# Two edits at the end of a two-layer block: the last chunk of the experts turned on TensorE, and token arrays stored in DRAM as they lie in SBUF

## The chip, the cores and the metric

The kernel runs on one core of one Trainium2 chip. A core has five engines, each with its own queue of instructions, worked through in order: TensorE (PE in the profile; PEld is its weight load), VectorE (DVE), ScalarE (ACT), GpSimd (POOL) and SyncE (SP), which here mostly issues DMAs. The on-chip memories are SBUF (128 partitions) and PSUM, where TensorE writes its results. DRAM is reached by DMA only, over 16 DMA engines that all queues share. The metric is the device time in microseconds of one execution.

## The reference, cut to what matters

The input `x` has 8 sequences of 512 tokens of 256 features. The block has two layers, each adding to `x` the sum of an attention and a second part, both fed from the normalised `xn`.

```python
xn = _layernorm(x, axis=-1)
x = x + _L0_attn_ref(xn, ...) + _L0_ffn_ref(xn, ...)     # causal attention; gated feed-forward, 1024 wide
xn = _layernorm(x, axis=-1)
x = x + _L1_attn_ref(xn, ...) + _L1_ffn_ref(xn, ...)     # attention with position bias; experts
```

The experts of layer 1, where the larger edit lies:

```python
grouped = x.reshape(x.shape[:-2] + (-1, ne, d))              # groups of 16 tokens
logits = jnp.einsum('...btd,des->...btes', grouped, controller)
perm = (logits + tie == max over the 16 tokens of the group) # one token per group, expert and slot
sel = jnp.einsum('...btd,...btes->...besd', grouped, perm)   # the token picked: 64 (expert, slot) pairs
inner = jax.nn.relu(jnp.einsum('...besd,desf->...besf', sel, f1) + bias)   # 256 -> 64
inter = jnp.einsum('...besf,esfd->...besd', inner, f2)                     # 64 -> 256
out = jnp.einsum('...besd,...btes->...btd', inter, perm)     # back to the token's place
```

All 64 pairs of expert and slot have weights of their own, so `inner` and `inter` are computed pair by pair over many groups, while `sel` and `out` go group by group over all pairs.

## The kernel before, in words

**Stages.** Layer 0's attention comes first, then the feed-forward of layer 0 (which also prepares the first sequence of layer 1), layer 1's attention, and the experts. Between the stages, and where SBUF is short, arrays lie in DRAM: `x1d` (x after layer 0's attention), `x2d` (after its feed-forward), `x3d` (after layer 1's attention), `xn1d` (layer 1's `xn`), and `xnd` and `xt1d` (`xn` of the two layers, transposed).

**Token arrays.** A sequence in SBUF is a tile of 128 partitions by 4 by 256: token `t * 128 + p` lies on partition `p`, at place `t`. `x1d`, `x2d`, `x3d` and `xn1d` are 4096 rows of 256 floats, token by token, so the 4 KB of a partition go to or come from four places of 1 KB each. `xnd` and `xt1d` are kept partition by partition, 4 KB in one piece. `fetch_x` (L82), `leave_x` (L86), the store of `xn1d` in `prep1` (L536), `fetch_xn` (L940) and the load of `x` in `combine` (L1118, two of the four places, 256 KB) move the token arrays. In one execution either arm of the feed-forward runs, and there are 8 stores of each array, 8 loads of `x1d`, 16 of `x2d`, 8 of `xn1d` and 16 half loads of `x3d`.

**The experts** go in four chunks of two sequences, 64 groups each (`NG`); the 64 pairs are 32 pairs of pairs (`NP`), two of 64 hidden features together filling 128 rows.

- `route(b)`: logits by TensorE, the maximum by VectorE, `perm` and its transpose `permT`.
- `gather(b)`: `sel`, features on partitions, by products with a block-diagonal `perm`.
- `up(ch)` (L1050): `inner` = relu of 64-wide products, 128 of them, over `sel`; the result is laid block-diagonally, so that one product holds two pairs.
- `go_down(ch)` (L1082): 32 products `d_ps` (L1092), 128 rows of (pair, group) by 256 features, evicted to `down`. Now rows stand by pair and group, and `combine` needs, for each group, all pairs on the partitions. The turn is made through DRAM: 8 stores `inter<-down` (L1102) and 8 loads `back<-inter` (L1108), each 512 KB.
- `combine(ch)` (L1110): for two token tiles at a time, loads `x` from `x3d`, 8 products `y_ps` (L1122) of `permT` with `back`, an addition (L1130), and the store to `out` (L1131).

**Buffers.** The pool `big` has one buffer for each tag: `sel` (read by `up`) and `back` (read by `combine`), 32 KB for each partition both. So `back` of a chunk is written only when the `combine` of the chunk ahead has read its own. In PSUM `ps_a` has 3 buffers, `ps_b` 3 and `ps_c` 2 (for `y_ps`); `x` in `combine` has 3 in SBUF. `evacuate` (L71) takes VectorE and ScalarE in turn.

**Order.** The attention stages are written in an order of their own, kept as written. In the experts, functions are generators interleaved by `by_turns`; a scheduler then sets the order of the instructions on each engine. Of `up(3)` with `combine(2)`, and then `go_down(3)`, it makes on TensorE: `up(3)`, 18 products of `go_down(3)`, `combine(2)`, 14 products, `combine(3)`.

Of the kernel before, what the change touches and what calls it, by code (L numbers as in the profile page):

```python
# [2 lines left out]

# [1 line left out]

# [6 lines left out]
F32 = mybir.dt.float32  # L12
# [9 lines left out]
P = 128  # L22
B, S, D = 8, 512, 256
NT = B * S // P
TPB = S // P
# [37 lines left out]
def block_kernel(ctx: ExitStack, tc: tile.TileContext, a: dict, out: bass.AP):  # L63
# [7 lines left out]
    def evacuate(dst, src):  # L71

        turn[0] ^= 1
        if turn[0]:
            nc.vector.tensor_copy(dst, src)
        else:
            nc.scalar.copy(dst, src)
# [3 lines left out]

    def fetch_x(pool, b, src, tag="x", to=x):  # L82
        to[b] = pool.tile([P, TPB, D], F32, tag=tag, name="x")
        nc.sync.dma_start(to[b], src[b * S : (b + 1) * S, :].rearrange("(t p) d -> p t d", p=P))

    def leave_x(b, dst):  # L86
        nc.sync.dma_start(dst[b * S : (b + 1) * S, :].rearrange("(t p) d -> p t d", p=P), x[b])

    x1d = dram.tile([B * S, D], F32, name="x1d")
    x2d = dram.tile([B * S, D], F32, name="x2d")  # L90
    x3d = dram.tile([B * S, D], F32, name="x3d")
    xnd = dram.tile([B * P, 2 * S], F32, name="xnd")
    xn1d = dram.tile([B * S, D], F32, name="xn1d")
    xt1d = dram.tile([B * P, 2 * S], F32, name="xt1d")

    cst = cpool.tile([P, C_CAUSAL], F32, name="cst")
# [432 lines left out]
    def prep1(b, xn, pools, psum, tag, wqkv, bufs, evacuate):  # L529


        for t in range(TPB):
            normalise(1, b, t, xn[:, t, :], xn)
            if t % 2:
                yield
        nc.sync.dma_start(xn1d[b * S : (b + 1) * S, :].rearrange("(t p) d -> p t d", p=P), xn)  # L536
        yield
        yield from pause()
        xt = pools[0].tile([P, 2, S], F32, tag="xT", name="xT")
        for i in range(0, TPB, 2):  # L540
            yield from transpose_steps(
                [xn[:, i + j, :] for j in range(2)], xt[:, :, i * P : (i + 2) * P], psum, tag, evacuate
            )
        yield xt
        yield from pause()
        for m in range(2):
            for kind, dst, scale in ((0, qd1, -(HD**-0.5)), (1, kd1, 1.0)):
                cols = slice(kind * D + m * P, kind * D + (m + 1) * P)
                yield from project(
                    pools[1],  # L550
                    psum,
                    tag,
                    [(wqkv[:, k, cols], xt[:, k, :]) for k in range(2)],
                    scale,
                    dst[b, m],
                    (lambda: ready1.add((b, m))) if kind else None,
                    not kind,
                    bufs,
                )
# [371 lines left out]
    with ExitStack() as st:  # L931
# [7 lines left out]

        def fetch_xn(b):  # L940
            t = work.tile([P, TPB, D], F32, tag="xn", name="xn1")
            nc.sync.dma_start(t, xn1d[b * S : (b + 1) * S, :].rearrange("(t p) d -> p t d", p=P))
            return t

        def fetch_xt(b):
# [27 lines left out]
        inner = big.tile([P, NP, 2, NG], F32, name="inner")  # L973
        nc.gpsimd.memset(inner[:ES, :, 1, :], 0.0)
        nc.gpsimd.memset(inner[ES:, :, 0, :], 0.0)
        perms, permT, sel, back = {}, {}, {}, {}

        def route(b):

# [73 lines left out]
        def up(ch):  # L1053

            s = sel.pop(ch)
            for q in range(4):
                u_ps = ps_b.tile([P, NP // 4, NG], F32, tag="b", name="u_ps")
                for r in range(NP // 4):
                    for k in range(2):
                        for e in range(2):  # L1060
                            nc.tensor.matmul(
                                u_ps[e * ESZ : (e + 1) * ESZ, r, :],
                                lhsT=f1[q][:, k, (2 * r + e) * ESZ : (2 * r + e + 1) * ESZ],
                                rhs=s[:, k, q * NP // 2 + 2 * r + e, :],
                                start=(k == 0),
                                stop=(k == 1),
                            )
                    if r % 2:
                        yield
                at = slice(q * NP // 4, (q + 1) * NP // 4)  # L1070
                raw = work.tile([P, NP // 4, NG], F32, tag="raw", name="raw")
                nc.vector.tensor_tensor(raw, u_ps, fbias[:, at].unsqueeze(2).to_broadcast([P, NP // 4, NG]), ALU.add)
                yield
                for e in range(2):
                    half = slice(e * ES, (e + 1) * ES)
                    nc.scalar.activation(inner[half, at, e, :], raw[half], AF.Relu)
                yield
# [3 lines left out]
        def go_down(ch):  # L1081

            back[ch] = big.tile([P, NG // 2, D], F32, tag="back", name="back")
            for r0 in range(0, NP, NR):
                if r0 % NH == 0:
                    half = dram.tile([P, NH, D], F32, name=f"inter{ch}_{r0}")
                down = work.tile([P, NR, D], F32, tag="down", name="down", bufs=3)
                for r1 in range(0, NR, 2):
                    d_ps = ps_b.tile([P, 2, D], F32, tag="b", name="d_ps")
                    for i in range(2):  # L1090
                        r = r0 + r1 + i
                        nc.tensor.matmul(  # L1092
                            d_ps[:, i, :],
                            lhsT=inner[:, r].rearrange("p e g -> p (e g)"),
                            rhs=f2[r // (NP // 4)][:, r % (NP // 4), :],
                            start=True,
                            stop=True,
                        )
                    yield
                    evacuate(down[:, r1 : r1 + 2, :], d_ps)  # L1100
                    yield
                nc.sync.dma_start(half[:, r0 % NH : r0 % NH + NR, :], down)  # L1102
                if (r0 + NR) % NH == 0:
                    by_group = half.rearrange("(e g h) r d -> h e r g d", e=2, h=2)
                    for h in range(2):
                        for e in range(2):
                            at = h * ES + 2 * (r0 + NR - NH) + e
                            nc.sync.dma_start(back[ch][at : at + 2 * NH - 1 : 2], by_group[h, e])  # L1108

        def combine(ch):  # L1110

            rows, pt = back.pop(ch), permT.pop(ch)
            for i in range(2):
                b = 2 * ch + i
                for t in range(0, TPB, 2):
                    at = slice(b * S + t * P, b * S + (t + 2) * P)
                    xr = work.tile([P, 2, D], F32, tag="x", name="x", bufs=3)
                    nc.sync.dma_start(xr, x3d[at, :].rearrange("(t p) d -> p t d", p=P))  # L1118
                    y_ps = ps_c.tile([P, 2, D], F32, tag="y", name="y_ps")
                    for j in range(2):  # L1120
                        for q in range(4):
                            nc.tensor.matmul(  # L1122
                                y_ps[32 * q : 32 * q + 32, j, :],
                                lhsT=pt[:, i, (t + j) * P + 32 * q : (t + j) * P + 32 * q + 32],
                                rhs=rows[:, (i * TPB + t + j) * 4 + q, :],
                                start=True,
                                stop=True,
                            )
                        yield
                    nc.vector.tensor_add(xr, xr, y_ps)  # L1130
                    nc.sync.dma_start(out[at, :].rearrange("(t p) d -> p t d", p=P), xr)  # L1131
                    yield

        def by_turns(*works):
            works = deque(w for w in works if w is not None)
            while works:
                w = works.popleft()
                try:
                    next(w)
                    works.append(w)  # L1140
                except StopIteration:
                    pass

        def chain(*works):
            for w in works:
                yield from w
# [3 lines left out]
        by_turns(chain(gather(0), gather(1)))  # L1150
        for ch in range(chunks):
            more = ch + 1 < chunks
            by_turns(
                up(ch),
                chain(
                    *([route(2 * ch + 2), route(2 * ch + 3)] if more else []),
                    *([combine(ch - 1)] if ch else []),
                ),
            )
            by_turns(go_down(ch), chain(gather(2 * ch + 2), gather(2 * ch + 3)) if more else None)  # L1160
        by_turns(combine(chunks - 1))


# [51 lines left out]
```

## Time and profile before

The program was timed three times: 2200.61, 2200.88 and 2191.32 us, median 2200.61.

| | |
|---|---|
| time of the profiled execution | 2195.91 us |
| its span in the profile | 2194.2 us |
| instructions | 29805 |
| TensorE busy | 1930.5 us, 88% of the span |
| VectorE, ScalarE, GpSimd busy | 1337.9, 938.8, 610.1 us |
| DMA packets, bytes | 151905, 254.40 MB |
| the experts' stage | about 1940 to 2194 us |
| `up(3)` ends on TensorE | 2124.0 us |

All times in the profile count from the span's start. An engine that is busy most of the span isn't the bound in every stage; the chain of waits, followed back from the last instruction, shows which work or transfer each stretch waited for. The page's rows of tenths give the busy share of each of 40 slices of 55 us. The granted clock is that of TensorE as a share of full speed. Products of f32 appear as two records each in the trace, transposes as one.

### The profile page before, as it was taken

What the parts mean: (1) busy time and instruction counts of PE and PEld (TensorE: products, weight loads), DVE (VectorE), ACT (ScalarE), POOL (GpSimd) and SP (SyncE); (2) the same over time, 40 slices, a digit from 0 to 9 for tenths busy, and PEclk for the clock granted to TensorE, in tenths of its full rate; (3) what the DMA queues carried; (4) which work ended last, traced back from release to release, by engine and by line L of the source; (5) the groups of instructions that cost most, each with busy time, mean ns of one, the idle gap of its engine ahead of it and who ended that gap; (6) DMA issues with size and microseconds to landing.
All of it is one profiled execution on the core that took longest, in us unless ns stands there. A gap on an engine that the chain in (4) does not pass through costs nothing.

```text
span 2194.2 us, 29805 instructions
## 1 busy us (share of the span) xinstructions
PE 1930.5 (88%) x10182; PEld 1259.3 (57%) x10182; DVE 1337.9 (61%) x3621; ACT 938.8 (43%) x1570; POOL 610.1 (28%) x552
## 2 busy tenths in 40 slices
PE   3689999999799999999999779999999999968863
PEld 1345555555488888888888544544544444436652
DVE  3667776677345535535535367888878878735431
ACT  0244444445322212212222137777777778834320
POOL 4211111112100000000000256656656657732200
PEclk8799999999899999999999879999999999989986
DMA  5647767674430000000001384554553554167697
GB/s 126 177 121 175 185 164 195 174 173 109 181 127 30 20 10 29 20 1 20 20 1 49 90 238 98 117 124 91 116 127 89 114 121 77 47 235 204 192 254 204
DMA packets 151905, 254.40 MB, mean 116 GB/s; under 512 B 14382, under 2 KB 84911, under 8 KB 151395
## 3 DMA queue, kind: packets, MB, share of 16 engines
q1 hardware_dynamic: 146418, 245.56, 43.2%
q10 hardware_dynamic: 4864, 6.24, 0.9%
q8 instruction: 82, 1.34, 0.3%
q0 software_dynamic: 464, 0.63, 0.1%
q14 instruction: 77, 0.62, 0.1%
HBM read 171.58 MB, written 91.29 MB: 120 GB/s over the span
## 4 chain that ended last, share of the span: by engine, by line
PE 62%; DMA 12%; DVE 10%; ACT 4%; issue 4%; POOL 1%; SPq 1%; ACTq 1%; POOLq 0%; DVEq 0%
PE hid_ps L780 21%; PE t_ps L338 7%; PE ctx_ps L385 7%; PE s_ps L287 6%; PE proj_ps L522 3%; DMA qs<-rows 3%; DVE junk L299 3%; DMA ks<-kd 3%; PE val L780 3%; PE gate L780 3%; PE ffo L780 2%; PE o_ps L443 2%; DMA back<-inter 1%; DMA inter<-down 1%; PE d_ps L1092 1%
## 5 line engine op out<-in xcount | busy, mean ns | idle before, releaser
L287 PE MATMUL s_ps<-ks,qs 96*128 96x512 f32 (+2 forms) x1024 | 471.0, 468 | 81.6 <-DMA ks<-kd 40.4
L351 POOL TENSOR_TENSOR pt<-pt,bias 128x512 f32<-128x512 f32 x320 | 408.8, 1288 | 242.5 <-ACT pt L350 233.5
L338 PE MATMUL t_ps<-qs,ks 128*128 128x512 f32 (+2 forms) x1024 | 394.8, 391 | 38.1 <-DMA qs<-rows 15.1
L299 DVE CUSTOM_DVE_ANT_0 junk<-s_ps,bias 128x512 f32<-128x512 f32 x512 | 338.0, 686 | 120.3 <-PE s_ps L287 107.2
L287 PEld LDWEIGHTS s_ps<-ks,qs 96*128 96x128 f32 x1024 | 201.9, 198 | 265.6 <-DVE least L299 110.7
L299 DVE CUSTOM_DVE_ANT_0 junk<-s_ps,mask 128x384 f32<-128x384 f32 (+3 forms) x512 | 233.1, 486 | 142.0 <-PE s_ps L287 140.8
L338 PEld LDWEIGHTS t_ps<-qs,ks 128*128 128x128 f32 x1024 | 197.9, 195 | 149.1 <-ACT pt L350 43.2
L376 ACT ACTIVATE pt<-pt 128x1024 f32<-128x1024 f32 x256 | 273.7, 1069 | 3.2 <-POOL pt L351 3.1
L770 DVE CAST h<-hf 128x512 fp32r<-128x512 f32 x192 | 81.2, 426 | 303.2 <-ACT hf L819 302.2
L385 PE MATMUL ctx_ps<-pt,vst 128*32 128x512 f32 (+3 forms) x2048 | 262.5, 533 | 3.7 <-ACT pt L376 2.5
L819 ACT ACTIVATE hf<-hid_ps,sh 128x512 f32<-128x512 f32 x128 | 88.1, 688 | 380.5 <-PE hid_ps L780 374.6
L350 ACT COPY pt<-t_ps 128x512 f32<-128x512 f32 x320 | 184.3, 585 | 151.8 <-PE t_ps L338 150.3
L780 PE MATMUL hid_ps<-h,h1T_m 128*128 128x512 f32 x1024 | 237.4, 391 | 0.0
L780 PE MATMUL hid_ps<-h,h2T_m 128*128 128x512 f32 x1024 | 236.9, 392 | 0.0
L780 PEld LDWEIGHTS hid_ps<-h,h2T_m 128*128 128x128 f32 x1024 | 192.2, 188 | 42.6 <-issue 2.9
L780 PEld LDWEIGHTS hid_ps<-h,h1T_m 128*128 128x128 f32 x1024 | 191.2, 188 | 43.8 <-DVE h L771 2.5
L128 POOL TENSOR_TENSOR r<-ve,power 128x4 f32<-128x4 f32 x16 | 16.2, 1012 | 706.9 <-DVE ve L125 602.9
L363 POOL TENSOR_SCALAR_AFFINE_SELECT pt<-pt 128x512 f32<-128x512 f32 x128 | 81.7, 639 | 404.6 <-ACT pt L353 229.6
L353 ACT ACTIVATE pt<-t_ps 128x512 f32<-128x512 f32 (+1 forms) x256 | 130.3, 546 | 99.9 <-PE t_ps L338 95.0
L348 DVE TENSOR_TENSOR pt<-t_ps,bias 128x512 f32<-128x512 f32 x192 | 131.6, 685 | 15.4 <-PE t_ps L338 14.0
L771 DVE TENSOR_TENSOR h<-hf,h 128x512 fp32r<-128x512 f32 x192 | 132.0, 690 | 5.6
L355 ACT ACTIVATE pt<-t_ps 128x256 f32<-128x256 f32 (+1 forms) x128 | 61.9, 491 | 148.3 <-PE t_ps L338 117.1
(137 smaller groups left out, 2265.2 us busy)
## 6 DMA issues: line engine op xcount, KB each, us to landing
qs<-qd SPq DMA_DIRECT2D x128, 256.0 KB
ks<-kd SPq DMA_DIRECT2D x64, 256.0 KB
ks<-kd SPq DMA_DIRECT2D x128, 128.0 KB
inter<-down SPq DMA_DIRECT2D x32, 512.0 KB
back<-inter SPq DMA_DIRECT2D x32, 512.0 KB
qd<-hi SPq DMA_DIRECT2D x32, 256.0 KB
qd<-lo SPq DMA_DIRECT2D x32, 256.0 KB
kd<-hi SPq DMA_DIRECT2D x32, 256.0 KB
```

Source lines behind the costliest of these rows:

```text
L287: nc.tensor.matmul(ps[:, :n], lhsT=job["qs"][:ROW_M, r, c * P : (c + 1) * P], rhs=job["ks"][:ROW_M, r, :n], start=True, stop=True,)
L299: nc.vector.tensor_tensor_reduce(junk[:, :width], ps[:, :width], add, 1.0, 3e38, ALU.add, ALU.min, job["least"][:, c, r : r + 1])
L338: nc.tensor.matmul(ps[:, base - at : S - at], lhsT=job["ks"][:, r, j * P : (j + 1) * P], rhs=job["qs"][:, r, base:], start=True, stop=True,)
L348: nc.vector.tensor_tensor(pt[:, r, :], ps, bias, ALU.add)
L350: nc.scalar.copy(pt[:, r, :], ps)
L351: nc.gpsimd.tensor_tensor(pt[:, r, :], pt[:, r, :], bias, ALU.add)
L353: nc.scalar.activation(pt[:, r, lo:], ps[:, lo:], AF.Exp, scale=-1.0)
L376: nc.scalar.activation(pt, pt, AF.Exp, scale=-1.0)
L385: nc.tensor.matmul(job["ctx"][32 * r : 32 * r + 32, lo:], lhsT=job["v"][:, j, r, :], rhs=job["p"][j][:, r, lo:], start=(j == 0), stop=(j = ...
L771: nc.vector.tensor_tensor(t[1][:, k, :], value, t[0][:, k, :].bitcast(F32), ALU.subtract)
L780: nc.tensor.matmul(ps, lhsT=l, rhs=r, start=(i == 0), stop=(i == len(pairs) - 1))
L819: nc.scalar.activation(hf, ps, AF.Gelu, scale=scales[sc][:, o : o + 1])
```

## The change

**The last chunk** (`ch` = 3) no longer goes through DRAM. `go_down_here` computes the products the other way round: weights `f2` stationary, `inner` moving (128 columns: two pairs of 64 groups), two halves of 128 features, so 64 products of 128 columns in place of 32 of 256. The result has features on partitions; its evictions write it to `dn` with the pairs innermost, in the buffer of `sel`, which `up(3)` has read by then. `turn_here` transposes 128 by 128 blocks of `dn` on TensorE (64 transposes, 16 groups of four in a PSUM buffer of `ps_a`), which gives rows by (group of two, pair) with features along, and evicts them to `back`. `combine` draws these steps as it goes, 12 before its first tile and 8 before the others. `combine(2)` is now chained behind `go_down_here(3)` in place of beside `up(3)`. The other chunks are as before.

**The layouts.** `x1d`, `x2d`, `x3d` and `xn1d` become 1024 rows (sequence, partition) of 1024 floats, as the tiles lie in SBUF; `tokens` picks the view by the array's width, so the input `x` and the output keep theirs.

```diff
     def fetch_x(pool, b, src, tag="x", to=x):
         to[b] = pool.tile([P, TPB, D], F32, tag=tag, name="x")
-        nc.sync.dma_start(to[b], src[b * S : (b + 1) * S, :].rearrange("(t p) d -> p t d", p=P))
+        nc.sync.dma_start(to[b], tokens(src, b))
...
+    def tokens(src, b):
+
+        if src.shape[1] == D:
+            return src[b * S : (b + 1) * S, :].rearrange("(t p) d -> p t d", p=P)
+        return src[b * P : (b + 1) * P, :].rearrange("p (t d) -> p t d", d=D)
+
+    x1d = dram.tile([B * P, TPB * D], F32, name="x1d")
+    x2d = dram.tile([B * P, TPB * D], F32, name="x2d")
+    x3d = dram.tile([B * P, TPB * D], F32, name="x3d")
...
+    xn1d = dram.tile([B * P, TPB * D], F32, name="xn1d")
...
+        def go_down_here(ch):
+
+            dn = turned[ch] = big.tile([P, 2, NG, ES], F32, tag="sel", name="dn")
+            for r0 in range(0, NP, 4):
+                for d in range(2):
+                    d_ps = ps_b.tile([P, 8, NG], F32, tag="b", name="d_ps")
+                    for r in range(r0, r0 + 4):
+                        nc.tensor.matmul(
+                            d_ps[:, 2 * (r - r0) : 2 * (r - r0) + 2, :],
+                            lhsT=f2[r // (NP // 4)][:, r % (NP // 4), d * P : (d + 1) * P],
+                            rhs=inner[:, r],
+                            start=True,
+                            stop=True,
+                        )
+                        if r % 2:
+                            yield
+                    evacuate(dn[:, d, :, 2 * r0 : 2 * r0 + 8], d_ps.rearrange("p s g -> p g s"))
+                    yield
+
+        def turn_here(ch, rows):
+
+            dn = turned.pop(ch)
+            for g0 in range(0, NG // 2, 2):
+                i_ps = ps_a.tile([P, 2, D], F32, tag="a", name="i_ps")
+                for q in range(2):
+                    for d in range(2):
+                        nc.tensor.transpose(
+                            i_ps[:, q, d * P : (d + 1) * P],
+                            dn[:, d, 2 * (g0 + q) : 2 * (g0 + q) + 2, :].rearrange("p g s -> p (g s)"),
+                            ident,
+                        )
+                yield
+                evacuate(rows[:, g0 : g0 + 2, :], i_ps)
+                yield
+
         def combine(ch):
 
-            rows, pt = back.pop(ch), permT.pop(ch)
+            pt = permT.pop(ch)
+            if ch in turned:
+                rows = big.tile([P, NG // 2, D], F32, tag="back", name="back")
+                steps = turn_here(ch, rows)
+            else:
+                rows, steps = back.pop(ch), iter(())
...
-                    nc.sync.dma_start(xr, x3d[at, :].rearrange("(t p) d -> p t d", p=P))
+                    nc.sync.dma_start(xr, tokens(x3d, b)[:, t : t + 2, :])
+
+                    for _ in islice(steps, 8 if i or t else 12):
+                        yield
...
-            by_turns(go_down(ch), chain(gather(2 * ch + 2), gather(2 * ch + 3)) if more else None)
+            if more:
+                by_turns(
+                    up(ch),
+                    chain(route(2 * ch + 2), route(2 * ch + 3), *([combine(ch - 1)] if ch else [])),
+                )
+                by_turns(go_down(ch), chain(gather(2 * ch + 2), gather(2 * ch + 3)))
+            else:
+                by_turns(up(ch))
+                by_turns(chain(go_down_here(ch), combine(ch - 1)))
         by_turns(combine(chunks - 1))
```

## The prediction

> **What bounds the kernel now.** I read the whole page first, then the end of the chain of waits in order of time, since the change's larger part lies in the last chunk of the experts (L1150 on). Of the page two lines matter.
>
> ```profile
> PE 62%; DMA 12%; DVE 10%; ACT 4%; issue 4%; POOL 1%; SPq 1%; ACTq 1%; POOLq 0%; DVEq 0%
> PEclk8799999999899999999999879999999999989986
> ```
>
> TensorE carries the kernel as a whole, but the last slices show a lower granted clock: it idles there. The chain from 2114.8 us on (start us, length us, what):
>
> ```profile
> 2114.84 10.99 DMA inter<-down
> ...
> 2128.85 10.31 DMA back<-inter
> 2139.16 0.24 issue
> 2139.40 6.10 PE y_ps L1122 x64
> ...
> 2155.18 7.87 DMA inter<-down
> ...
> 2163.95 3.03 DMA inter<-down
> ...
> 2169.01 11.66 DMA back<-inter
> 2180.66 0.24 issue
> 2180.91 5.00 PE y_ps L1122 x48
> ...
> 2187.11 2.72 DMA x<-x3d
> 2190.02 0.69 DVE x L1130
> ```
>
> Read: the DRAM round trip of chunk 2 ends at 2139.16, and `combine(2)` follows it. That of chunk 3 runs from 2155.18 to 2180.66 with nothing beside it; then `combine(3)`, whose last `x` row had to be fetched (2.72). TensorE's own timeline shows what it did meanwhile (start, length, line, operation, idle before):
>
> ```profile
> 2115.03 3.95 PE L1061 MATMUL u_ps<-sel,f 128*64 128x64 f32 x128 [0.56 <-issue]
> 2123.71 0.33 PE L1061 MATMUL u_ps<-sel,f 128*64 128x64 f32 x2 [4.73 <-issue]
> 2123.97 9.76 PE L1092 MATMUL d_ps<-f,inner 128*128 128x256 f32 x36
> 2139.40 6.10 PE L1122 MATMUL y_ps<-back,permT 128*32 128x256 f32 x64 [5.68 <-DMA back<-inter]
> 2145.43 6.31 PE L1092 MATMUL d_ps<-f,inner 128*128 128x256 f32 x28
> 2180.91 5.83 PE L1122 MATMUL y_ps<-back,permT 128*32 128x256 f32 x64 [29.17 <-DMA back<-inter]
> ```
>
> `up(3)` ends at 2123.97, 70.2 us before the span's end at 2194.2. In these 70.2 us TensorE works 28 us. `go_down(3)` is cut in two at 2133.7, because `combine(2)` stands inside it in the queue and waits for its rows.
>
> **The change part by part. 1: the last chunk without DRAM.** The built program of the changed kernel keeps TensorE's, VectorE's, ScalarE's and GpSimd's order up to the end of `up(3)`; SP's order up to there is the same too, with other shapes. From there TensorE has: 64 products `d_ps` (128 wide in place of 32 of 256), 12 transposes `i_ps`, all 32 `y_ps` of `combine(2)`, then 52 transposes with the 32 `y_ps` of `combine(3)` between them. (A product of f32 takes two records of the trace, a transpose one.) SP loses 8 stores `inter<-down` and 8 loads `back<-inter`, 8 MB. No DMA is added.
>
> The new path from 2123.97, term by term:
>
> *The products.* 24 records of `d_ps` 256 wide took 5.32 us on the chain at 2031.06: 0.222 each. A record half as wide is half of that, 0.111, if its weight load stays hidden; the four 128-wide transposes `ct_ps` at 1931.39 take 0.63 us in all, the first to land after 0.30 by the mean of that group, so (0.63 - 0.30) / 3 = 0.11 each with a weight load of the same size. So 128 x 0.111 = 14.2 us. The clock is half at first, after the 4.73 us of waiting. In the windows view (last three columns: granted clock, DMA share, GB/s):
>
> ```profile
> 2124.00:2125.00 1.00, 1.00 (x4) 0.82 (x4) 0.69 (x1) 0.14 (x1) 0.00 (x0) 0.50 1.03 382
> 2127.00:2128.00 1.00, 1.00 (x5) 0.83 (x5) 0.00 (x0) 0.36 (x1) 0.00 (x0) 0.84 0.71 184
> 2128.00:2129.00 1.00, 1.00 (x6) 0.73 (x5) 0.50 (x1) 0.22 (x1) 0.00 (x0) 1.00 1.09 251
> ```
>
> The 36 records of before show the price: 9.76 us less 36 x 0.222 = 1.8. So 16.0 us, to 2139.9. The 16 evictions `dn<-d_ps` have the form of `sel<-g_ps` (0.69 on VectorE, 0.59 on ScalarE), alternate, and a tile takes TensorE 0.89: they hide, all but the last. Lower bound of the products 14.2 (warm), upper 128 x 0.197 = 25.2, if each waited for its weight load of 197 ns; I take 16.0, by the transposes.
>
> *Last eviction and first three groups of transposes.* Every transpose needs all of `dn`: 0.8. Then 12 x 0.11 and 0.2 to land: 1.5. To 2142.2.
>
> *`combine(2)`.* Its rows landed at 2139.16 before and nothing of that transfer changes, so it starts without a wait. 64 records took 3.82 us at 2043.41 with the clock at 1.00, and 6.10 at 2139.40, after idleness. It follows 18 us of work: I take 3.8, upper end 6.1. To 2146.0.
>
> *Transposes with `combine(3)`.* The evictions into `back` must wait until `combine(2)` has read the only buffer, and the three `ps_a` buffers are full: 0.85 until the first is free. TensorE then has 52 x 0.11 + 64 x 0.06 = 9.6 us. VectorE has 8 evictions and 5 additions at 0.69, 9.0 us, in an order of its own: close behind. At the end the last transpose has to be evicted before the last `y_ps` (0.85). 1.0 for waits on `x`: with three buffers a load waits for an `out` to land (2.6 at 2045.27), then takes 2.7 itself, against some 2.8 us per tile of TensorE. Sum 12.3, to 2158.3. Upper end: four loads missed by 2.7 each, 23.
>
> *The end.* From the last addition to the span's end took 4.2 us (2190.02 to 2194.2), with 0.1 of handing over. New end 2162.6, so **-31.6 us**. With all lower ends (products 14.2, no waits on `x`, no 0.8) it is -35; with all upper ends (25.2, 6.1, 23) it would be -9, but these don't go together.
>
> **2: the layouts.** 72 transfers of 512 KB or their equal (8 + 8 for `x1d`, 8 + 16 `x2d`, 8 + 8 `x3d`, 8 + 8 `xn1d`) go from runs of 1 KB to 4 KB (2 KB in `combine`). Nearest rows: loads of `f1` (4 KB runs) and of `f2` (1 KB runs) with the engines full:
>
> ```profile
> 1952.00:1954.00 2.00, 0.46 (x4) 0.33 (x4) 2.00 (x5) 0.00 (x0) 0.64 (x1) 0.81 1.03 410
> 1964.00:1966.00 2.00, 1.80 (x7) 0.81 (x6) 2.00 (x4) 1.40 (x4) 1.63 (x2) 1.00 1.11 349
> ```
>
> 410 against 349 GB/s is 0.23 us per 512 KB, 16 us of DMA time over all 72. Nearly all of it lies beside TensorE-bound work with the DMA engines 0 to 70% busy (the page's row of tenths). Only where the queue is full, from 2044 on, does it count: 4 loads of `xn` and 8 half loads of `x` before `up(3)`, 1.8 us; some of that is in slack. I take -1.6. Bounds: 0 and -16; a loss has no row for it, since `xnd`, `xt1d` and `inter` have these long runs already. SP issues a load of the one shape in 0.36 us (`x<-x1d`, median), of the other in 0.33 (`xT<-xnd`).
>
> **Sum:** -31.6 - 1.6 = -33.2. The profiled execution took 2195.9, so 2162.7; I say 2163. The shown runs' median, 2200.6, lies 4.7 higher; they spread by 9.6 (0.4%), so 0.5% is about what can be told from no change.
>
> [...] Row: transposes before always stand among products, so the trace cannot say whether they alone hold the clock at 1.00. [...]
>
> **The rivals.**
>
> *A, the forecast.* Chance 0.62: 2163, own range 2156 to 2170.
>
> *B, the clock falls to 0.50 in the last phase.* For it: it fell in every gap before a `y_ps` (0.50 at 2139 and 2181), and the mix has small waits. Against: all those gaps were over 4 us. Price: `y_ps` of both chunks 6.1 for 3.8 (4.6 more) and 64 transposes at 0.22 (7.0 more); some hides behind VectorE's 9.0. About +10: 2173. Chance 0.12.
>
> *C, TensorE waits for its instructions, or for `x`.* Waits called issue, 0.56, 4.73, 2.22, stand after runs of about 128 pairs of weight load and product, with the DMA queues full; the new tail has 322 pairs where 192 were. Against: those 128 ran in 4 us; here they take 10 to 16. Price: one such wait, 2 to 5 us, or three late loads at 2.7: 2169. Chance 0.10.
>
> *D, the layouts are worth more.* For it: from 2110 to 2139 the DMA share is about 1, and `hi` waited 37.7 us for `xn<-xn1d` in three waits. Against: `back<-inter`, the slow one at about 200 GB/s, stays. Half of the 16 us: 2155. Chance 0.11.
>
> *E, slower.* One mechanism: long runs on SP's queue hold up `qs<-rows` in layer 1, which is 3% of the chain, about 66 us over the kernel. Layer 1 has 32 jobs; 33 us / 32 = 1.0 us more per job decides. Against: near the end of layer 1, `x3d` stores and `x` loads are issued after a job's rows, with over 10 us till the next. With 2 us per job: +31, 2227. Chance 0.03.
>
> *F, about equal:* unhidden weight loads (+9), B (+10), four late loads (+11) and nothing from the layouts (+2) would take 32 of the 33 us; I see no reason for all at once. 2195. Chance 0.02.
>
> **How the numbers follow.** Range 2151 to 2177: it holds A, B and C and most of D. Faster by over 0.5% (under 2189.6): A to D, 0.95. Within: 0.02. Slower: 0.03.
>
> **What will show it.** After `up(3)`: a run of 128 `d_ps` records in about 16 us without a break; 12 transposes; `y_ps` x64 with no wait for `back<-inter`; no idle of TensorE over 3 us; no `inter<-down` in the last 40 us; clock 1.00 to the end (else B). `up(3)` should end 0 to 3 us sooner than at 2123.97 (more is D). The prediction is wrong if `d_ps` takes over 20 us, if VectorE's additions wait for `x<-x3d` at each tile, or if layer 1 or the feed-forward changes by more than 5 us.

## The result, and the profile after

The changed kernel takes 2163.6 us (median of four, 2159.0 to 2167.6) against 2197.5 before: a ratio of 0.985, 95% interval 0.982 to 0.988, 33.9 us between the medians. The prediction was 2163, range 2151 to 2177. The profiled execution took 2159.0 us, the fastest of the four, with a span of 2157.3.

These are the page's lines of after; the last slices now have the clock near full.

```profile
PE 65%; DVE 11%; DMA 10%; issue 5%; ACT 4%; POOL 2%; SPq 1%; ACTq 1%; POOLq 0%; DVEq 0%
PEclk8799999999999999999999969999999999999989
DMA packets 119905, 246.03 MB, mean 114 GB/s; under 512 B 14125, under 2 KB 43694, under 8 KB 119394
```

The last of these lines as it was before:

```profile
DMA packets 151905, 254.40 MB, mean 116 GB/s; under 512 B 14382, under 2 KB 84911, under 8 KB 151395
```

DMA packets fell from 151905 to 119905 and bytes by 8.4 MB, the round trip of chunk 3; packets under 2 KB fell from 84911 to 43694, most of that by the new layouts (48046 with the layouts alone, 80559 with the last chunk's edit alone).

The end of the chain of waits of the changed kernel (start us, length us, what):

```profile
2105.32 7.61 PE u_ps L1068 x254
2112.93 4.65 issue
2117.58 0.47 PE u_ps L1068 x2
2118.05 16.36 PE d_ps L1124 x128
2134.43 0.59 ACT dn L78
2135.07 1.20 PE i_ps L1143 x9
2136.27 3.79 PE y_ps L1172 x64
2140.08 0.59 ACT back L78
...
2140.72 1.53 PE i_ps L1143 x12
2142.25 1.00 PE y_ps L1172 x16
2143.25 1.46 PE i_ps L1143 x12
2144.71 0.55 PE y_ps L1172 x2
2145.26 0.59 PE i_ps L1143 x4
...
2151.45 1.32 PE y_ps L1172 x16
2152.80 0.69 DVE x L1180
```

From the end of `up(3)` at 2118.05 to the last addition no DMA stands in the chain. The stretch to the end of the span is 39.3 us, where it was 70.2. The rest of the difference between the two profiles lies ahead of it: `up(3)` ends 5.9 us sooner. How much of that is the layouts' and how much differs from run to run is the question of the first two experiments.

### The profile page after: what moved, and what is told of

Read it like the earlier page. It is cut to its first block, busy times and chain, and to the rows that moved or that the text cites. A ratio compares the mean times of both kernels' runs of the same rounds, so it can differ in the third digit from the quotient of the medians.

```text
span 2157.3 us, 30027 instructions
## 1 busy us (share of the span) xinstructions
PE 1933.1 (90%) x10310; PEld 1264.2 (59%) x10310; DVE 1341.9 (62%) x3629; ACT 943.2 (44%) x1578; POOL 610.1 (28%) x552
## 2 busy tenths in 40 slices
DMA packets 119905, 246.03 MB, mean 114 GB/s; under 512 B 14125, under 2 KB 43694, under 8 KB 119394
## 3 DMA queue, kind: packets, MB, share of 16 engines
q8 instruction: 83, 1.36, 0.3%
## 4 chain that ended last, share of the span: by engine, by line
PE 65%; DVE 11%; DMA 10%; issue 5%; ACT 4%; POOL 2%; SPq 1%; ACTq 1%; POOLq 0%; DVEq 0%
PE hid_ps L787 21%; PE t_ps L345 7%; PE ctx_ps L392 7%; PE s_ps L294 6%; PE proj_ps L529 4%; DMA qs<-rows 4%; DMA ks<-kd 3%; DVE junk L306 3%; PE val L787 3%; PE gate L787 2%; PE ffo L787 2%; PE o_ps L450 2%; PE d_ps L1099 1%; PE u_ps L1068 1%; PE g_ps L1046 1%
```

## The experiments

My theory was that the last chunk's edit is worth 31 us, the layouts 1 to 2, and that the new tail is bounded by TensorE at full clock. Against it stood: that the layouts are worth the whole 5.9 us; that a phase rich in transposes would lose the clock; and, for versions that go further, that what TensorE waits for in the waits called issue has nothing to do with DMA.

**The changed kernel again, without an edit.**

> The changed kernel once more, beside the three others. All theories: about 33 us faster than before, ratio 0.984 to 0.986. Its profile shows whether up(3) again ends near 2118 us (in the kernel before it ended at 2124.0) or whether that moves from run to run.

Ratio 0.984 (0.981 to 0.987), median 2160.4 against 2197.8. In its profile `up(3)` ends at 2112.8, 5.2 us sooner than in the first profile of the same program, and the tail takes 39.0 us. So the place of `up(3)` moves by some 5 us from run to run, and the 5.9 us of two single traces prove nothing; the tail's length is steady. Part of the movement arises far ahead of the experts: in the eight traces with `x1d` in its new layout, whose kernels do not differ up to there, the last store of `x1d` was issued anywhere from 572.6 to 587.2 us.

**The layouts alone.** The loop over the chunks is put back:

```diff
             else:
-                by_turns(up(ch))
-                by_turns(chain(go_down_here(ch), combine(ch - 1)))
+                by_turns(up(ch), combine(ch - 1))
+                by_turns(go_down(ch))
```

> Only the four token arrays' layouts are changed; the last chunk goes through DRAM as before. Theory (layouts are hidden nearly everywhere): -1.6 us, between 0 and -3, ratio 0.9985 to 1.000; up(3) ends at 2121 to 2124, and from there to the end it takes 70 us as before. Rival (the 5.9 us by which up(3) ends sooner in the changed kernel are the layouts'): -6 us, ratio 0.997.

Ratio 0.9979 (0.9962 to 0.9996): 4.6 us of 2197.8, from 0.9 to 8.4. (The medians, 2197.8 and 2191.2, lie 6.6 apart.) The ratio lies below the theory's 0.9985 to 1.000 and nearer the rival's 0.997, but the interval holds 0.9985, 1.6 us and the rival's 6 us alike: that the layouts bring something is shown, how much is not. `up(3)` ended at 2118.2, and from there to the end it took 70.6 us, as before.

**The last chunk alone.**

```diff
-    x1d = dram.tile([B * P, TPB * D], F32, name="x1d")
+    x1d = dram.tile([B * S, D], F32, name="x1d")
...
```

(and likewise `x2d`, `x3d`, `xn1d`)

> Only the last chunk is turned on TensorE; the token arrays keep their old layout. Theory: -31 us, ratio 0.9855 to 0.987, and 39 us from the end of up(3) to the end of the span. Rival (the layouts bring 6): -27 to -28 us, ratio 0.9875; the tail would still be 39 us.

Ratio 0.9854 (0.9825 to 0.9882), 32.1 us faster, 26 to 38. From the end of `up(3)` (2121.7) to the end of the span (2161.4) 39.7 us. By the ratios the two edits add up, within their intervals: 32.1 and 4.6 against 35.4 for both on the same chip. This edit holds two moves, the turn on TensorE and `combine(2)` behind the products in place of among them, and no run takes them apart. In the trace before, TensorE waited 5.68 us for the rows of `combine(2)` and 29.17 us for those of `combine(3)`.

**Many transposes and nothing else.** Forty groups of four transposes of `dn`, which nobody reads, ahead of the real ones:

```diff
             dn = turned.pop(ch)
+            for n in range(40):
+                w_ps = ps_a.tile([P, 2, D], F32, tag="a", name="w_ps")
+                for q in range(2):
+                    for d in range(2):
+                        g = 2 * (2 * n + q) % NG
+                        nc.tensor.transpose(
+                            w_ps[:, q, d * P : (d + 1) * P], dn[:, d, g : g + 2, :].rearrange("p g s -> p (g s)"), ident
+                        )
```

> 160 transposes of dn that nobody reads are put between the products of the last chunk and its own transposes, with nothing else on TensorE beside them. Theory (transposes keep the clock up as products do): 160 x 0.11 = 17.6 us more, granted clock 1.00 throughout. [...]

TensorE's timeline of this run, and below it two stretches of its windows view (last three columns: granted clock, DMA share, GB/s):

```profile
2126.16 15.99 PE L1124 MATMUL d_ps<-inner,f 128*128 128x128 f32 x128
...
2142.82 17.36 PE L1144 MATMUL w_ps<-ident,dn 128*128 128x128 f32 x157 [0.24 <-ACT dn L78]
2160.01 1.47 PE L1151 MATMUL i_ps<-ident,dn 128*128 128x128 f32 x12
2161.42 3.81 PE L1180 MATMUL y_ps<-back,permT 128*32 128x256 f32 x64
```

```profile
2156.00:2158.00 2.00, 2.00 (x21) 2.00 (x20) 0.00 (x0) 0.00 (x0) 0.00 (x0) 1.00 0.00 0
2162.00:2164.00 2.00, 2.00 (x44) 0.94 (x33) 1.27 (x2) 0.00 (x0) 0.00 (x0) 1.00 0.00 0
```

Three of the 160 transposes stand ahead of the last eviction of `dn`; the other 157 took 17.36 us, 0.11 each. The granted clock was 1.00 from 2130 us on, to their end and after. The tail from the end of `up(3)` at 2126.2 took 56.3 us, 17.0 more than 39.3. So the fall that rival B feared did not come: f32 transposes alone held a clock that was up (at B's price of 0.22 each the 157 would have taken 34.5 us). Whether they would bring it up from half this run does not show, as it was full when they began.

**Chunk 2 without its round trip.**

```diff
             back[ch] = big.tile([P, NG // 2, D], F32, tag="back", name="back")
+            if ch == 2:
+                nc.gpsimd.memset(back[ch], 0.0)
...
+                if ch == 2:
+                    continue
                 nc.sync.dma_start(half[:, r0 % NH : r0 % NH + NR, :], down)
```

> The changed kernel without the DRAM round trip of chunk 2 (16 DMAs of 512 KB left out, back of chunk 2 is set to zero instead), so that up(3) runs with an almost idle DMA queue. Asked: what TensorE waits for in the 4.7 to 5.3 us called issue, two records before the end of up(3). Theory (its instructions come late because the DMA queues are full): the wait falls under 1 us and the products after it start at full clock, 14.3 us in place of 16.4. Rival (the wait belongs to that place in the program, whatever the queues do): 4 to 5 us as before, and half clock after it.

TensorE's timeline of this run (the first line is from `up(2)`), a stretch of its `up(3)`, and that stretch of the changed kernel:

```profile
2074.44 1.26 PE L1068 MATMUL u_ps<-sel,f 128*64 128x64 f32 x35 [1.46 <-issue]
...
2104.98 8.08 PE L1068 MATMUL u_ps<-sel,f 128*64 128x64 f32 x256
2112.99 14.56 PE L1128 MATMUL d_ps<-inner,f 128*128 128x128 f32 x128
```

```profile
2106.00:2112.00 6.00, 6.00 (x213) 6.00 (x210) 2.08 (x3) 2.52 (x4) 0.00 (x0) 1.00 0.02 5
```

```profile
2106.00:2112.00 6.00, 6.00 (x212) 6.00 (x210) 2.92 (x5) 2.62 (x5) 0.00 (x0) 1.00 1.11 231
2112.00:2118.00 6.00, 1.35 (x34) 1.10 (x29) 0.00 (x0) 1.16 (x2) 0.00 (x0) 0.76 1.09 285
```

With the DMA engines idle (share 0.02 in place of 1.11) all 256 records of `up(3)` run through without a break, and the products after them take 14.56 us in place of 16.4, since the clock has not fallen (granted 1.00 from 2110 to 2125 us here, 0.50 from 2118 to 2121 in the changed kernel). In the same trace `up(2)`, which keeps chunk 1's round trip beside it, had its wait called issue, 1.46 us (2.00 in the changed kernel, at a share of 1.13 from 2058 to 2060 us). And in the last kernel below, where chunk 2 has no round trip either, `up(3)`, with products of `combine(2)` between its own, ran with a share of 0.52 (2150 to 2160 us) and without such a wait. So at the end of `up(3)` the wait of 4.65 us came with the traffic of chunk 2 and was gone without it. Traffic does not always bring one: `up(2)` of that last kernel shows no wait called issue, at a share of 1.07 (2060 to 2070 us). That it is the fetch of TensorE's instructions fits: in the traces with two breaks they are 128 pairs of weight load and product apart, which is 256 instructions, and the page's q8, kind instruction, moved 83 packets and 1.36 MB, 16 KB each. If that queue serves TensorE alone, this is 248 of its 20620 records to a packet, by estimate, near the 256 between the breaks. With the share at 1.09 (2112 to 2118 us in the changed kernel) the wait was 4.65 us, with half clock behind it: the 128 products behind it took 15.99 to 16.79 us in six traces, 1.4 to 2.2 more than here. That it is the fetch that waits is argued from these counts; no run shows it directly. The order of chunk 2's own products changed too in this kernel, so the breaks could stand at other places; but 256 pairs in a row hold two places that are 128 pairs apart, wherever they begin. Its total (2167.6, one execution) says nothing on the change, because `combine(2)` then waited 9.1 us for the zeros, which GpSimd wrote late.

**Only `x1d` in the new layout**, with the last chunk turned on TensorE (`x2d`, `x3d` and `xn1d` as before).

> The last chunk turned on TensorE, and of the four token arrays only x1d in its new layout. From the last store of x1d to the first load of x2d for layer 1 the two traces with the old layout show 583.6 and 584.0 us, those with the new one 581.2 to 582.0. Theory (the gain there is x1d's, whose store and first load stand ahead of the feed-forward's first weights): 581 to 582. Rival (it is x2d's, whose stores run beside the feed-forward): 583 to 584.

572.60 to 1154.55: 581.95 us, within the new layout's range and outside the old one's. The end mark itself holds some `x2d`: its first load comes 3.1 us after the `x2d` store ahead of it in the old layout, here too, and 2.7 to 2.9 us in the new one. So `x1d` brings nearly all of it and `x2d` some 0.3 us, which isn't in the chain of waits; but this is one trace, and two later kernels with all layouts new took 582.7. The parts stand in the chain of waits, here of the kernel before and then of this one:

```profile
578.47 3.31 DMA x1d<-x
...
582.27 8.25 DMA w2T_m<-w2T_c
590.52 0.04 issue
590.57 2.08 PE val L780 x4
592.64 1.71 PE gate L780 x4
594.35 1.17 PE val L780 x4
595.51 0.93 PE gate L780 x4
```

```profile
572.60 2.93 DMA x1d<-x
576.04 8.02 DMA w2T_m<-w2T_c
584.10 2.08 PE val L787 x4
586.18 0.93 PE gate L787 x4
587.11 0.92 PE val L787 x4
```

The last store lands 0.4 us sooner, and the first weights, queued behind the load of `x1d`, 0.2 (0.5 in the changed kernel, 7.71; over all traces 8.25 and 8.60 with the old layout, 7.71 to 8.02 in seven with the new one). The rest is the clock: after the wait for the weights TensorE starts at half clock (granted 0.50 from 590 to 594 us before, from 587 to 589 in the changed kernel), and how many groups it does so differs from run to run (before: three slow ones; here: one; in the last kernel below, with the new layouts too, three again, and 582.7 us). So under 1 us of the 2 is the transfers' for certain; the ramp's part is not settled.

**The load of `x1d` behind the weights.**

```diff
-                fetch(0)
+                fetch(0, False)
...
+                fetch_x(xin, 0, x1d)
+
                 def parts(t, k, value):
```

(`fetch` gets a second argument, which leaves out `fetch_x`; the load stands after the weight loads.)

> The changed kernel with the feed-forward's first load of x1d put behind the weight loads on SP's queue instead of ahead of them. Theory (that load delays the first weights by its own time in the queue): w2T lands about 1.3 us sooner (6.4 us after its issue in place of 7.7), and the whole is 1 to 2 us faster than the changed kernel, ratio to before 0.983 to 0.984. Rival (the weights are slow by themselves): no difference.

Ratio 0.9838 (0.9816 to 0.9860), against 0.9839 (0.9814 to 0.9865) for the changed kernel: no difference that can be told, and intervals of 5 us to either side could not have told the 1 to 2 us that were expected. In its profile the weights land 7.24 us after their issue, 0.5 sooner than 7.7 rather than 1.3, but four groups then ran slow (2.08, 1.71, 1.71, 1.29), and the way from the last `x1d` store to the first `x2d` load took 582.7 us. In this trace the clock's ramp took back what the transfer gave.

**Chunk 2 turned on TensorE as well.** `dn` of chunk 2 takes the buffer of `sel`, so `gather(3)` comes after the turn:

```diff
+        def turn_now(ch):
+
+            back[ch] = big.tile([P, NG // 2, D], F32, tag="back", name="back")
+            yield from turn_here(ch, back[ch])
...
-                by_turns(go_down(ch), chain(gather(2 * ch + 2), gather(2 * ch + 3)))
+                if ch + 2 < chunks:
+                    by_turns(go_down(ch), chain(gather(2 * ch + 2), gather(2 * ch + 3)))
+                else:
+                    by_turns(go_down_here(ch))
+                    by_turns(turn_now(ch))
+                    by_turns(chain(gather(2 * ch + 2), gather(2 * ch + 3)))
             else:
-                by_turns(up(ch))
-                by_turns(chain(go_down_here(ch), combine(ch - 1)))
+                by_turns(up(ch), combine(ch - 1))
+                by_turns(go_down_here(ch))
```

(`combine` takes chunk 2's rows from `back`.)

> Chunk 2 is turned on TensorE as well; its dn lies in the buffer of sel, so gather(3) starts only when it has been turned. TensorE gets 64 more transposes (7 us), the round trip that combine(2) waited for goes, and combine(2) moves ahead of the last products. Theory (the end is TensorE's now, so 7 us of transposes are paid for by 3.8 us of combine(2) and about 5 us of waits that go): -5 to +2 us against the changed kernel, 2157 to 2164, ratio to before 0.981 to 0.985. Rival (a stage without DMA beside it stands still at each hand-over between gather, up and down): 5 to 10 us slower than the changed kernel.

Ratio to before 0.9993 (0.9966 to 1.0019): about 33 us slower than the changed kernel, far outside both. The chain of waits and SP's queue (from its timeline) show why:

```profile
2099.12 0.70 DVE dn L76
2099.86 1.17 PE d_ps L1124 x8
2101.06 0.59 ACT dn L78
2101.70 1.17 PE d_ps L1124 x8
2102.89 0.69 DVE dn L76
2103.58 1.21 DVE down L76 x2
2104.81 2.94 DMA inter<-down
...
2109.18 9.75 DMA back<-inter
2118.93 2.76 issue
2121.69 5.96 PE y_ps L1172 x64
```

```profile
2061.04 44.08 SPq L1109 DMA_DIRECT2D inter<-down  x4
```

The scheduler put the last two evictions `down<-d_ps` of chunk 1 behind the eight `dn<-d_ps` of chunk 2 on VectorE. So chunk 1's last stores waited on SP for 44 us, its round trip ended at 2118.9, and TensorE stood 15.0 us ahead of `combine(1)`. And two of the three `ps_b` buffers were held by those evictions, so the products of chunk 2 and their evictions took turns: 1.9 us for each tile in place of 0.91, 29.6 us for sixteen in place of 14.56. The two losses, 15 us each, make 30 of the 33. My rival spoke of standstills at hand-overs; the trace puts it down to one order on one queue. Whether a version with that order mended would gain was not tried; its last `d_ps` did run at 14.56 us without a wait before them.

## Why the prediction was right, point by point

- *The tail.* Predicted 38.6 us from the end of `up(3)` in place of 70.2; measured 39.3, and 39.0 to 39.7 in four more traces. Terms: products 16.0, measured 16.4; last eviction and first transposes 2.3, measured 1.9 (2134.4 to 2136.3); `combine(2)` 3.8, measured 3.79, with no wait for `back<-inter`; transposes with `combine(3)` 12.3, measured 12.7 (2140.1 to 2152.8); the end 4.3, measured 4.5. The 12.7 came near by luck in part, since two errors cancel. TensorE's own work there was put at 9.6 and took 12.1 without a wait: 52 transposes 6.7 in place of 5.7, 64 records of `y_ps` 5.4 in place of 3.8, where the two alternate in short pieces (two records of `y_ps` took 0.55, four transposes 0.59); why a short piece costs more, no run shows. Against it, 1.0 for waits on `x` and 0.85 for the last eviction did not come on TensorE. That the products' weight loads stay hidden, and that the ramp costs 1.8 us, held: 14.56 us without the ramp.
- *The wait on `x`* inside the last phase came once, 0.8 us, and the chain doesn't show it.
- *The layouts.* Predicted 1.6 us, measured 4.6 (0.9 to 8.4). The interval holds the 1.6, so the total does not prove the term wrong; the traces show what it left out. Fewer and longer runs did come (125280 packets with the layouts alone in place of 151905), and the transfers named below took less time, but the term took only the experts' stage as exposed. "Nearly all of it lies beside TensorE-bound work" missed the borders between stages, where the transfer itself is the chain: the last `x1d` store, 0.4 us (3.31 before, 2.93 with `x1d` alone); the first weights behind the load of `x1d`, 0.2 to 0.5 in the traces shown; and the half-clock ramp after them, 1.0 to 1.3 between the traces shown, though two others with the new layouts ramped nearly as slowly as before (5.5 and 6.0 us for the first four groups, 5.9 before). The last `x3d` store, 2.90 us before and 2.62 after, adds 0.3. From the first load of `xt` after it to the end of `up(3)` the two old-layout traces give 183.3 and 186.8 us, and four new-layout ones from 179.9 to 184.1: on average 2.4 less, but that spread is as large, so the experts' share stays open.
- *The rivals.* B, the clock falling in the last phase, did not come: 1.00 from 2122 to TensorE's last product. C, waits on instructions in the tail, did not come either: the longest wait of TensorE after `up(3)` was 0.7 us, for an eviction. (C counts 322 pairs in the new tail; by the prediction's own counts, 128 records of `d_ps`, 64 transposes and 128 records of `y_ps`, they are 320.) D had half a point at most: the layouts may be worth more, but the three waits of `hi` for `xn<-xn1d` that it named, 37.7 us before, were 37.9 in the changed kernel. E (layer 1 held up by longer runs): from its first load of `x2d` to its last store of `x3d` layer 1 took 774.7 and 773.3 us with the old layout and 770.5 to 777.3 in seven traces with the new one; the kernel with only `x1d` new took 779.0. That spread is far below the 31 us of E, so layer 1 was not held up by longer runs; a loss of 2 or 3 us could not be seen in it. F did not come.
- *"`up(3)` should end 0 to 3 us sooner"* was a poor sign to look for: in repeated traces of one program it moved by 5 us.

## What to carry to other kernels

A round trip through DRAM cost TensorE 5.68 us of waiting here while other work stood beside it and 29.17 us in the last turn of the loop; there it paid to do the last turn by another method, some 8 us of transposes for 25 us of transfers, while the same method one turn earlier lost about 33 us, and needs the engines' orders to be looked at first. The layouts' gain, as far as it could be located, lay at the borders between stages, where a store, a load and the first weights follow one another with nothing beside them (0.4, 0.3 and 0.2 to 0.5 us): such borders are the first place to look, and the sum of DMA time did not show it. To compare parts of two single traces, take lengths from mark to mark that repeat over several runs, not positions.

## What the runs showed that I had not expected

- TensorE's wait called issue at the end of `up(3)` came with chunk 2's round trip: 4.65 to 5.28 us two records before the end in all eight traces that have it (DMA share 1.07 from 2118 to 2124 us before, 1.09 from 2112 to 2118 in the changed kernel), none in the trace with the engines idle (0.02) and none in the one with a share of 0.52; and 1.4 to 2.2 us lost to half clock behind it.
- F32 transposes alone held the granted clock at 1.00 over 17 us.
- Half a microsecond less of waiting ahead of a TensorE stage was outweighed by the ramp in one trace (7.24 us for the weights in place of 7.71): one to four groups ran slow after waits of 7.2 to 8.6 us for the weights, a difference of up to 2.2 us (6.8 us for the first four groups with the late load of `x1d`, 4.6 in the changed kernel).
